# Squares in the common product tiles; 32 products left over, V1 x and V0 x of two chunk pairs together in one group

## The chip, the cores and the metric

The kernel runs on one core of a Trainium2 chip. The metric is the device time of one execution in microseconds: 444.65 us before the change (the median of three runs, 444.37, 444.65 and 445.27). Everything is float32. TensorE multiplies, VectorE (DVE), ScalarE (ACT) and GpSimd (POOL) prepare its operands and finish its results, and SyncE (SP) issues most of the DMAs.

## The reference

A compressed interaction network: three cross layers of 128 channels over F = 64 features with E = 16 numbers each, for B = 1024 examples. After the first two layers half of the channels go to the output and half go on.

```python
for i in range(n):
    z = jnp.einsum('bfe,bge->bfge', x0, h)        # x0 = x, h = x at first
    z = z.reshape(Bn, f0 * fh, e)
    y = jnp.einsum('oc,bce->boe', Ws[i], z) + bs[i][None, :, None]
    if split_half and i != n - 1:
        half = y.shape[1] // 2
        x_i, h = (y[:, :half, :], y[:, half:, :])
    else:
        x_i, h = (y, y)
    xs.append(x_i)
pooled = jnp.sum(jnp.concatenate(xs, axis=1), axis=2)
return pooled @ fc_w.T + fc_b
```

Only one number for each example comes out, so the layers collapse. The channels that go on from the first layer are h1 (64 sums of products x_f·x_g, with W0). The second and third layers together are worth, per example, the sum of h1 · (q/QS), where q are 64 sums of the same products x_f·x_g with weights M that come from V2 = fc·W2 and W1, plus a term in V1 x. The channels of the first layer that go straight to the output are x · (V0 x + cx). So a kernel needs all products x_f·x_g of a column, 64 sums of them for h1 and 64 for q, and two small 64×64 products with x itself, V1 x (it belongs to q) and V0 x.

## The kernel before, in words

**Columns and chunks.** A chunk is 32 examples × 16 numbers = 512 columns (N). There are 32 chunks; pair k is chunks 2k and 2k+1. Chunks 2, 3, 0, 1 (HEAD) start while weights are still being made, 4 and 5 are worked singly (`contract`), and the 13 pairs k = 3 to 15 follow in windows of 31 labels (SPAN) each. The q part of chunks 2 and 3 is left for the end.

**Products.** On partition p, tile t = (j, i) of a chunk holds x_f·x_g with f = (p + i) mod 64 and g = (p + 16(p//64) + 4(j+1)) mod 64, for i and j from 0 to 3. The differences g − f run over 1 to 32. So each unordered pair of two different features occurs once, those with difference 32 twice (half of their weights are set to zero), and the squares not at all. DVE makes four tiles in one instruction, `product` and `w_product` (lines L242 and L654): xa, four shifted copies of x, times xb, one shifted copy. Many xb are first copied to a PSUM bank by ACT (`second`, L568), into one of the two "y" banks.

**A pair of chunks a and b.** One 128-row tile times 64 columns of weights fills half of the array for one 512-column product; in the text a *slot* is the whole array for one such product, two matmuls side by side. For a pair the kernel does not work 4 × 16 such products, but a scheme like Strassen's and Winograd's with seven groups of eight. The operands T3, X, B21, B22 come from DVE (`make_pair`), the sums T2, T1, T4 from GpSimd (`w_mix`, L671; one of them by an accumulating DMA, L669). The groups add into banks named alpha, delta and beta (`p1_run`, `p7_run`, `w_run`, `p4_run`, `late_run`); between groups ACT copies partial sums out of a bank (`snap_p1` L682, `snap_u2` L685, `snap_p7` L688), and DVE adds them back at the end (`w_hb` L692, `w_qa` L696, `w_ha` L699), multiplies h by q (`w_uu` L702) and sums over the 16 numbers (`sums` L307).

**The extras.** What the common tiles lack is done with a tile e for each chunk, x in its lower 64 partitions (loaded a second time, `load_e`) and the squares x² in the upper ones (ACT, `square`, L178). Each chunk has
- `q_extra`: e (128 rows) times va or vb, V1 and the squares' weights for q, half a slot; scattered among the fills of a window (`first_fill`, `late_run`),
- `h_extra`: x² (64 rows) times the squares' weights for h1 (`w0ds`), 64×64, a quarter of a slot,
- `v0x`: x times v0, 64×64, a quarter of a slot; then `x_v0x` (L303) or `x_v0x_parts` (L776) on DVE.

The 64-row ones are gathered: in windows where chunk a leads (`a_leads`, every second one) `joint_squares` works the eight 64×64 products of two pairs at label 16.9 of the window, two slots with 64-row tiles. That makes six joint groups; pairs 0 and 2 have theirs in the head at label 28.1, pair 15 and chunks 2 and 3 theirs at the end (`squares`, `end_squares`).

**What sets the order.** It is written out by hand: `at(label, job)` collects jobs, and they are issued sorted by label, whatever their engine; a label is about one slot of TensorE. Each engine works its own instructions in that order and waits only for what it reads or overwrites. PSUM has eight banks in three pools: "acc" (4), "set" (2) and "y" (2). All matmuls issued through `mm` have line L540. The weights v0, va and vb are made on the chip in the head: GpSimd weighs (`weigh`, L551), DVE sums (`add_up`, L555), ACT puts the halves in place (`place`, L560).

Of the kernel before, what the change touches and what calls it, by code (L numbers as in the profile page):

```python
# [58 lines left out]
NV = 196  # L59
SQ = slice(96, 128)  # L60
# [10 lines left out]
def cin_kernel(ctx, tc, xra, xrb, wh, w0r, w1h, w2t, wx1, wx0, vec, lin, out):  # L71
# [7 lines left out]
    halves = [slice(0, F), slice(F, 128)]  # L79

# [23 lines left out]
    fcb, w0ds, fcr = vs[:, 3:4], vs[:, 4:68], vs[:, 68:196]  # L104

    misc = ps.tile([128, N], F32, tag="acc", name="misc", bufs=4)
# [22 lines left out]
    va, vb, v0 = (const_tile(n, [128, F]) for n in ("va", "vb", "v0"))  # L129
# [6 lines left out]
    xas, xbs, xxs, es = {}, {}, {}, {}  # L136
# [22 lines left out]
    def load_e(c):  # L159
        es[c] = sp.tile([128, N], F32, tag="e", name=f"e_{c}", bufs=4)  # L160
        nc.sync.dma_start(out=es[c][halves[0]], in_=xra[c, 0:F])

    def load_xx(k):
        xxs[k] = sp.tile([128, N], F32, tag="xx", name=f"xx_{k}")
        for n in range(2):
            nc.sync.dma_start(out=xxs[k][halves[n]], in_=xra[2 * k + n, 0:F])

    def copy_x(c):
        k, h, x = c // 2, halves[c % 2], xas[c][:, 0, :]
        if k not in xxs:  # L170
            xxs[k] = sp.tile([128, N], F32, tag="xx", name=f"xx_{k}")
        es[c] = sp.tile([128, N], F32, tag="e", name=f"e_{c}", bufs=4)
        nc.scalar.activation(es[c][halves[1]], x[halves[1]], AF.Square)
        nc.scalar.copy(es[c][halves[0]], x[halves[0]])
        nc.scalar.copy(xxs[k][h], x[h])

    def square(c):
        nc.scalar.activation(es[c][halves[1]], es[c][halves[0]], AF.Square)  # L178
# [32 lines left out]
    def shifted(c, j, tag):  # L211
        xbs.setdefault(c, {})[j] = ps.tile(
            [128, N], F32, tag=tag, name=f"xp_{c}_{j}", bufs=4 if tag == "acc" else 2
        )
# [10 lines left out]
    w0p = ps.tile([128, 2, NJ, F], F32, tag="set", name="w0p")  # L225
# [9 lines left out]
    def new_acc(c, n=N, tag="acc"):  # L235
        accs[c] = ps.tile([128, n], F32, tag=tag, name=f"acc_{c}", bufs=4 if tag == "acc" else 2)
# [127 lines left out]
    for n in range(2):  # L364
        pv = ps.tile([128, 512], F32, tag=("set", "y")[n], name=f"pv2_{n}")
# [13 lines left out]
    for h in range(2):  # L379
# [10 lines left out]
        ps.tile([128, N], F32, tag=tag, name=f"pm_{m}", bufs=4 if tag == "acc" else 2)  # L390
# [12 lines left out]
    pcx = ps.tile([128, 1], F32, tag="acc", name="pcx", bufs=4)  # L403
# [33 lines left out]
    xb2 = ps.tile([128, N], F32, tag="set", name=f"xp_{c2}_{NJ - 1}")  # L437
    nc.scalar.copy(xb2, xbs[c2][NJ - 1])
    xbs[c2][NJ - 1] = xb2
    for j in (0, 1):  # L440
        xb3 = ps.tile([128, N], F32, tag="y", name=f"xp_{c3}_{j}")
        nc.scalar.copy(xb3, xbs[c3][j])
        xbs[c3][j] = xb3
# [17 lines left out]
    ms = flat(msb).rearrange("p (v t g) -> p v t g", v=2, g=F)  # L461

# [8 lines left out]
    def read_columns(j, queue, half):  # L471
        queue.dma_start(
            out=ms[halves[half], 1, j * NI : (j + 1) * NI],
            in_=skewed(0, 16 * half + 4 * (j + 1), [[row, NI], [1, F]]),
        )

    def read_rows(js, queue, half):
        queue.dma_start(
            out=ms[halves[half], 0].rearrange("p (j i) g -> p j (i g)", i=NI)[:, js],
            in_=skewed(  # L480
                16 * half + 4 * (js.start + 1), 0, [[4 * row, js.stop - js.start], [1, NI * F]]
            ),
        )
# [17 lines left out]
    nc.sync.dma_start(out=va[halves[1]], in_=m_ap(0, 0, [[row + F, F], [1, F]]))  # L501
# [56 lines left out]
    def place(v, out, scale):  # L558
        for m in range(2):
            nc.scalar.activation(  # L560
                out[halves[0], 32 * m : 32 * m + 32],
                shift[halves[m], 32 * v : 32 * v + 32], AF.Identity, scale=scale,
            )


    def second(c, j):
        bank = ps.tile([128, N], F32, tag="y", name=f"xp_{c}_{j}")
        nc.scalar.copy(bank, xbs[c][j])  # L568
        xbs[c][j] = bank
# [5 lines left out]
    def q_extra(c, w, out=None):  # L575
        out = accs[c][halves[1 - c % 2]] if out is None else out[halves[c % 2]]
        mm(out, w, es[c])

    def h_extra(c, out=None, start=False):
        out = accs[c] if out is None else out  # L580
        mm(out[halves[c % 2]], w0ds[halves[1]], es[c][halves[1]], start=start)

    def new_y(k, tag):
        ys[k] = ps.tile([128, N], F32, tag=tag, name=f"y_{k}", bufs=4 if tag == "acc" else 2)

    def v0x(c, tag):
        if c // 2 not in ys:
            new_y(c // 2, tag)
        mm(ys[c // 2][halves[c % 2]], v0[halves[0]], es[c][halves[0]], start=True, stop=True)
# [22 lines left out]
    def w_bank(p, name, tag, bufs):  # L612
        if name not in p:
            p[name] = ps.tile([128, N], F32, tag=tag, name=f"{name}_{p['k']}", bufs=bufs)
        return p[name]

    def alpha(p):
        return w_bank(p, "alpha", "acc", 4)[p["A"]]

    def delta(p):  # L620
        return w_bank(p, "delta", "acc", 4)[p["O"]]

    def gamma(p):
        return w_bank(p, "alpha", "acc", 4)[p["O"]]

    def beta(p):
        return w_bank(p, "beta", "set", 2)[p["O"]]
# [53 lines left out]
    def snap_p1(p):  # L681
        nc.scalar.copy(snaps[0][p["O"]], alpha(p))  # L682

    def snap_u2(p):
        nc.scalar.activation(snaps[1][p["O"]], alpha(p), AF.Identity, bias=bh1[p["A"]])  # L685

    def snap_p7(p):
        nc.scalar.copy(snaps[2][p["A"]], delta(p))  # L688

    def w_hb(p):  # L690
        hb_ = snaps[2][p["A"]]
        nc.vector.scalar_tensor_tensor(hb_, alpha(p), bh1[p["A"]], hb_, ALU.add, ALU.add)  # L692

    def w_qa(p):
        q = snaps[0][p["O"]]
        nc.vector.tensor_tensor(q, beta(p), q, ALU.add)  # L696

    def w_ha(p):
        nc.vector.tensor_tensor(delta(p), delta(p), snaps[1][p["O"]], ALU.add)  # L699

    def w_uu(p, x, out, factor):
        nc.vector.scalar_tensor_tensor(  # L702
            uu[p[out], 0], x(p), 1.0 / QS, factor[p[out]], ALU.mult, ALU.mult
# [36 lines left out]
    def first_fill(p):  # L740
        return [(lambda: q_extra(p["a"], va, p["beta"]),)] + p4_run(p)[-LATE : -LATE // 2]
# [4 lines left out]
    def late_run(p, out=alpha, first=0, last=2 * NI):  # L746
        jobs = w_run(p, out, s4, "B22", out is gamma)[first:last]
        w = va if p["joint"] == 0 else vb
        return jobs if last < 2 * NI else jobs + [(lambda: q_extra(p["b"], w, p["alpha"]),)]

    def squares(p):
        a, b = p["a"], p["b"]
        h_extra(b, p["alpha"])
        h_extra(a, p["delta"])
        v0x(b, "set")
        v0x(a, "set")

    def joint_squares(q, p):
        a, b = q["a"], q["b"]
        h_extra(b, q["delta"], True)  # L760
        h_extra(a, q["delta"])
        v0x(b, "set")
        v0x(a, "set")
        a, b = p["a"], p["b"]
        h_extra(b, p["alpha"])
        h_extra(a, p["delta"])
        mm(p["delta"][p["A"]], v0[halves[0]], es[b][halves[0]], start=True)
        mm(p["alpha"][p["O"]], v0[halves[0]], es[a][halves[0]], start=True)

    def w_hb_squares(p):  # L770
        hb_ = snaps[2][p["A"]]
        nc.vector.tensor_tensor(hb_, p["delta"][p["A"]], hb_, ALU.add)

    def x_v0x_parts(p):
        for name, h in (("alpha", p["O"]), ("delta", p["A"])):
            nc.vector.scalar_tensor_tensor(  # L776
                uu[h, 1, :], p[name][h], cx[h], xxs[p["k"]][h], ALU.add, ALU.mult
            )
# [7 lines left out]
    def first_window(t, p, after, left):  # L786
        window(
            t, p,
            p1_run(p, GROUPS) + left[1][:1] + [(q_extra, 4, va)] + w_run(p, alpha, s2, "T2")
            + left[1][1:] + w_run(p, alpha, s1, "T3"),  # L790
            p7_run(p, GROUPS) + left[0][:1] + [(q_extra, 5, va)]
            + w_run(p, beta, wq_all, "B21", True, 2 * NI) + left[0][1:]
# [4 lines left out]
    def a_leads(t, p, before, after):  # L797
        fill = first_fill(before)
        window(
            t, p,  # L800
            p1_run(p, SECOND_ROW, False) + fill[:2] + w_run(p, alpha, s2, "T2", order=FIRST_ROW)
            + fill[2:] + w_run(p, alpha, s2, "T2", order=SECOND_ROW) + second_fill(before)
            + w_run(p, alpha, s1, "T3") + p7_run(after, FIRST_ROW),
            p7_run(p, GROUPS) + late_run(before) + w_run(p, beta, wq_all, "B21", True, 2 * NI)
            + p4_run(p)[:-LATE],
            4, 8, 15,
        )
        at(t + 16.9, joint_squares, before, p)

    def o_leads(t, p, before, after):  # L810
        last = after is None
# [5 lines left out]
            + w_run(p, beta, wq_all, "B21", True, 2 * NI)  # L817
            + (late_run(p, gamma, 0, NI) if last else p1_run(after, FIRST_ROW))
            + p4_run(p)[:-LATE],
            8, 4, 19,  # L820
        )
        if last:
            at(t + 30.2, squares, p)
# [347 lines left out]
```

## Time and profile before

| | us |
|---|---|
| runs | 444.37, 444.65, 445.27 |
| span of the profiled execution | 443.4 |
| PE busy | 439.8 (99%) |
| DVE busy | 401.4 (91%) |
| POOL busy | 371.9 (84%) |
| ACT busy | 117.7 (27%) |

The profile is of one execution. Its span goes from the first to the last instruction of the core; the time of a run has a little more around it. A line of a group names the line of the kernel, the engine, the operation and what it writes and reads by the program's tile names; "128*64 128x512" on a matmul is weights of 128 rows by 64 columns and a moving operand of 128 partitions by 512 columns. A float32 matmul leaves two records. PE is TensorE's matmul, PEld its weight load, which runs beside it.

### The profile page before, as it was taken

What the parts mean: (1) busy time and instruction counts of PE and PEld (TensorE: products, weight loads), DVE (VectorE), ACT (ScalarE), POOL (GpSimd) and SP (SyncE); (2) the same over time, 40 slices, a digit from 0 to 9 for tenths busy, and PEclk for the clock granted to TensorE, in tenths of its full rate; (3) what the DMA queues carried; (4) which work ended last, traced back from release to release, by engine and by line L of the source; (5) the groups of instructions that cost most, each with busy time, mean ns of one, the idle gap of its engine ahead of it and who ended that gap; (6) DMA issues with size and microseconds to landing.
All of it is one profiled execution on the core that took longest, in us unless ns stands there. A gap on an engine that the chain in (4) does not pass through costs nothing.

```text
span 443.4 us, 5939 instructions
## 1 busy us (share of the span) xinstructions
PE 439.8 (99%) x2228; PEld 159.0 (36%) x2228; DVE 401.4 (91%) x305; ACT 117.7 (27%) x216; POOL 371.9 (84%) x136
## 2 busy tenths in 40 slices
PE   9999999999999999999999999999999999999997
PEld 6333333336633333333333333333333333333345
DVE  4896799998998999999999999999999999999744
ACT  3155341232412123131312214131231313123211
POOL 5823898999998979899798979989798997989900
PEclk9999999999999999999999999999999999999999
DMA  8997997399769756895849868598567958592400
GB/s 283 404 373 193 359 409 290 125 324 232 269 130 342 170 189 232 179 347 119 288 145 260 268 153 307 121 313 210 182 234 186 346 119 282 189 265 71 95 1 0
DMA packets 35220, 99.86 MB, mean 225 GB/s; under 512 B 6420, under 2 KB 7220, under 8 KB 28728
## 3 DMA queue, kind: packets, MB, share of 16 engines
q1 hardware_dynamic: 31784, 84.67, 53.5%
q0 software_dynamic: 1872, 13.63, 16.8%
q10 hardware_dynamic: 1536, 1.18, 1.0%
q8 instruction: 17, 0.28, 0.3%
q14 instruction: 11, 0.09, 0.1%
HBM read 84.20 MB, written 1.64 MB: 194 GB/s over the span
## 4 chain that ended last, share of the span: by engine, by line
PE 94%; DMA 4%; SPq 1%; issue 0%; DVE 0%
PE alpha L540 43%; PE delta L540 23%; PE beta L540 11%; PE acc L540 7%; PE acc L250 4%; PE q L540 3%; DMA z<-in_w1h 3%; PE acc L283 3%; DMA z<-in_w0r 1%; SPq L143 1%; PE y L540 0%; SPq L193 0%; PE pm L396 0%; PE hx L540 0%; PE po L958 0%
## 5 line engine op out<-in xcount | busy, mean ns | idle before, releaser
L671 POOL TENSOR_TENSOR z<-z,z 128x2048 f32<-128x2048 f32 (+1 forms) x85 | 300.1, 3574 | 24.9 <-PE alpha L540 14.3
L654 DVE TENSOR_TENSOR z<-xa,xp 128x2048 f32<-128x2048 f32 x103 | 231.3, 2280 | 3.4 <-ACT xp L568 1.9
L540 PE MATMUL alpha<-z,ws 128*64 128x512 f32 x624 | 233.3, 593 | 0.0
L540 PEld LDWEIGHTS alpha<-z,ws 128*64 128x64 f32 x624 | 74.5, 137 | 89.4 <-issue 82.7
L540 PE MATMUL delta<-z,w_all 128*64 128x512 f32 x208 | 96.4, 592 | 0.0
L540 PE MATMUL alpha<-z,w_all 128*64 128x512 f32 x208 | 92.4, 592 | 0.0
L540 PE MATMUL beta<-z,w_all 128*64 128x512 f32 x208 | 91.7, 593 | 0.0
L540 PE MATMUL delta<-z,ws 128*64 128x512 f32 x208 | 91.4, 592 | 0.0
L568 ACT COPY xp<-xb 128x512 f32<-128x512 f32 x88 | 51.3, 585 | 128.5 <-DVE z L654 111.9
L242 DVE TENSOR_TENSOR z<-xa,xp 128x2048 f32<-128x2048 f32 (+2 forms) x29 | 43.3, 1546 | 2.6 <-ACT xp L568 1.7
L540 PEld LDWEIGHTS alpha<-z,w_all 128*64 128x64 f32 x208 | 28.5, 137 | 29.1 <-issue 27.7
L540 PEld LDWEIGHTS delta<-z,w_all 128*64 128x64 f32 x208 | 28.5, 137 | 28.7 <-issue 27.4
L540 PEld LDWEIGHTS delta<-z,ws 128*64 128x64 f32 x208 | 28.5, 137 | 28.6 <-issue 27.4
L540 PEld LDWEIGHTS beta<-z,w_all 128*64 128x64 f32 x208 | 28.0, 137 | 27.4 <-issue 25.7
L242 POOL TENSOR_TENSOR z<-xa,xb 128x2048 f32<-128x2048 f32 x6 | 27.3, 4569 | 11.1 <-DMA xb<-in_xrb 11.0
L540 PE MATMUL acc<-z,w_all 128*64 128x512 f32 x128 | 28.1, 592 | 0.0
L685 ACT ACTIVATE snap<-alpha,vs 64x512 f32<-64x512 f32 x13 | 8.9, 684 | 52.8 <-PE alpha L540 52.8
L250 PE MATMUL acc<-z,w_all 128*64 128x512 f32 x96 | 21.4, 596 | 0.0
L307 DVE TENSOR_REDUCE acc<-uu 128x64 f32<-128x1024 f32 (+2 forms) x19 | 19.6, 1036 | 0.2
L688 ACT COPY snap<-delta 64x512 f32<-64x512 f32 x13 | 7.5, 580 | 42.2 <-PE alpha L540 27.7
L660 DVE TENSOR_TENSOR xp<-xp,xb 128x512 f32<-128x512 f32 x26 | 18.1, 697 | 0.6
L242 POOL TENSOR_TENSOR z<-xa,xb_gps 128x512 f32<-128x512 f32 (+1 forms) x6 | 14.1, 2369 | 5.3 <-ACT xb_gps L321 4.4
(129 smaller groups left out, 368.4 us busy)
## 6 DMA issues: line engine op xcount, KB each, us to landing
xa<-in_xra SPq DMA_DIRECT2D x32, 1024.0 KB, 5.8
xb<-in_xrb SPq DMA_DIRECT2D x128, 256.0 KB, 7.6
z<-z POOLq DMA_DIRECT2D x13, 1024.0 KB, 8.1
e<-in_xra SPq DMA_DIRECT2D x28, 128.0 KB, 7.2
xx<-in_xra SPq DMA_DIRECT2D x28, 128.0 KB, 2.5
z<-in_w2t SPq DMA_DIRECT2D x2, 1024.0 KB, 11.9
z<-in_wx SPq DMA_DIRECT2D x2, 1024.0 KB, 9.9
xa<-in_xra SPq DMA_DIRECT2D x4, 256.0 KB
```

The lines of the kernel that those rows point to most:

```text
L143: queue.dma_start(out=xas[c][rows * n : rows * (n + 1), at, :], in_=bass.AP(tensor=xra.tensor, offset=c * XR * N + (at.start + rows * n) * ...
L242: engine.tensor_tensor(blocks[zs[c, j]][:, at, :], xas[c][:, at, :], xbs[c][j].unsqueeze(1).to_broadcast([128, last - first, N]), ALU.mult,)
L250: nc.tensor.matmul(accs[c][halves[i % 2]], w_all[:, j * NI + i, 0:64], blocks[zs[c, j]][:, i, :], start=(j == 0 and i < 2), stop=(j == las ...
L283: nc.tensor.matmul(accs[c][halves[1 - c % 2]], w_all[:, t, 64:128], blocks[zs[c, j]][:, i, :], start=(t == 0), stop=False, skip_group_chec ...
L307: nc.vector.tensor_reduce(acc[rows, of, k, half], uu[rows, of if at is None else at, E * half.start : E * half.stop].rearrange("p k (b e) ...
L540: nc.tensor.matmul(out, w, rhs, start=start, stop=stop, skip_group_check=True)
L568: nc.scalar.copy(bank, xbs[c][j])
L654: engine.tensor_tensor(blocks[b], xas[c], xbs[c][j].unsqueeze(1).to_broadcast([128, NI, N]), ALU.mult)
L660: nc.vector.tensor_tensor(bank, bank, xbs[p["b"]][j], ALU.add)
L671: nc.gpsimd.tensor_tensor(*(blocks[b][:, first:last] for b in (o, x, y)), ALU.subtract if in1 == "T3" else ALU.add,)
L685: nc.scalar.activation(snaps[1][p["O"]], alpha(p), AF.Identity, bias=bh1[p["A"]])
L688: nc.scalar.copy(snaps[2][p["A"]], delta(p))
```

## The change

- **Tiles.** The common tiles take g = (p + 16(p//64) + 4j + 3) mod 64. The differences now run over 0 to 31, with the squares among them (half of the weights of difference 0 are set to zero where they would count twice). What is left over is difference 32: 32 products x_d·x_{d+32}.
- **The far products.** For each pair one tile d holds, in quarters of 32 partitions, x shifted by 32 (`load_d`, `copy_d`); ACT copies it to a y bank (`far_bank`) and DVE multiplies it with xx, or with a copy xs whose halves are exchanged (`load_turned`), into d (`far_product`). Pairs with even k use xs and are called turned.
- **The extras of a pair** are V1 x twice (`along_x`, 64×64 on xx or xs), V0 x twice (64×64) and four products with d (`far`, 32×64: weights dh for h1 and dq or dqh for q). `joint_extras` does those of two pairs at label 15.9 of every second window: first the eight 64×64 ones in two slots, then the eight 32×64 ones in one. `plain_extras` does the V1 x and far ones of chunks 0, 1, 4, 5 at label 29.1, and their V0 x now stands alone at 24.1. `end_extras` does pair 15 and chunks 2 and 3 at label 6.9 of the end.
- **What goes:** the tiles e, their loads and squares, va, vb, `q_extra`, `h_extra`, `joint_squares`, `w_hb_squares`, `x_v0x_parts`, the memset of weights on DVE.
- **Banks.** PSUM banks are assigned by hand (`bank`, `pair_bank`). beta is now the other half of alpha's bank: `snap_p1` copies alpha there, and the B21 products add onto it, so there is no `w_qa`. h·q of a pair is one instruction over 128 rows (`w_uu`) where there were two over 64. Late (even) pairs collect the extras for q apart (`spare`, copied by ACT, `snap_spare`, and added by DVE, `w_qb`).
- **The head.** GpSimd fills a part of the weight tile with zeros and makes four 32×512 copies for pair 0's d before it waits for the q weights, and adds dq, dh and dqh later; v0 and v1 are placed by four ACT copies each (before, two for each of v0, va and vb); `add_up` of v0 stands 0.4 labels sooner, the product X of chunk 6 with j = 1 stands 0.8 later.

```diff
     def shift_pair(c, js):
-                at = 4 * (j + 1) + 16 * h
+                at = 4 * j + 3 + 16 * h
...
-    def load_e(c):
-        es[c] = sp.tile([128, N], F32, tag="e", name=f"e_{c}", bufs=4)
-        nc.sync.dma_start(out=es[c][halves[0]], in_=xra[c, 0:F])
+    def load_d(k):
+        if is_turned(k):
+            load_turned(k)
+        for n in range(2):
+            nc.sync.dma_start(
+                out=pair_tile(ds, "d", k)[halves[n ^ is_turned(k)]],
+                in_=xra[2 * k + n, 32 : 32 + F],
+            )
...
+    def far_bank(k):
+        xbs["d", k] = bank(f"d_{k}", "y")
+        nc.scalar.copy(xbs["d", k], ds[k])
+
+    def far_product(k):
+        x = (xds if k == 1 else xss if is_turned(k) else xxs)[k]
+        nc.vector.tensor_tensor(ds[k], xbs["d", k], x, ALU.mult)
...
     def snap_p1(p):
-        nc.scalar.copy(snaps[0][p["O"]], alpha(p))
+        nc.scalar.copy(beta(p), alpha(p))
...
-    def joint_squares(q, p):
-        a, b = q["a"], q["b"]
-        h_extra(b, q["delta"], True)
-        h_extra(a, q["delta"])
-        v0x(b, "set")
-        v0x(a, "set")
...
+    def joint_extras(q, p):
+        for r in (q, p):
+            along_x(r["b"], spare(r) if r["late"] else alpha(r), start=r["late"])
+            along_x(r["a"], beta(r))
+        for r in (q, p):
+            ys[r["k"]] = pair_bank(r, "y")
+            v0x(r["k"])
+        for r in (q, p):
+            far(r["b"], dh, 0, alpha(r) if r["late"] else spare(r), start=not r["late"])
+            far(r["a"], dh, 0, delta(r))
+        for r in (q, p):
+            far(r["b"], dqh if r["late"] else dq, 1, spare(r) if r["late"] else alpha(r))
+            far(r["a"], dq, 1, beta(r))
...
-        at(t + 16.9, joint_squares, before, p)
+        at(t + 15.9, joint_extras, before, p)
+        at(t + 24, snap_spare, p)
...
-            at(t + 1, load_e, c)
-            at(t + (10 if p["joint"] == 1 else 14), square, c)
+        early = p["k"] > 3
+        at(t - 8 if early else t + 1, load_d, p["k"])
+        far_pair(t + (6.9 if p["late"] else 17.5), p["k"])
...
-    for c in (0, 1, 4, 5):
-        at(28.1, v0x, c, "acc")
-        at(28.1, h_extra, c, None, c < 2)
-    zipped(30, [(q_extra, 0, va)], [(q_extra, 1, va)])
+    at(24.1, v0x, 0)
+    at(24.1, v0x, 2)
+    at(29.1, plain_extras)
...
-    g = (p % F + 16 * (p // F) + 4 * (t // NI + 1)) % F
+    g = (p % F + 16 * (p // F) + 4 * (t // NI) + 3) % F
```

More of the change, by code (lines that the diff above doesn't have):

```diff
@@ L168, in copy_x @@
-    def copy_x(c):
[L169 to L178, printed above, removed]
+            nc.sync.dma_start(out=pair_tile(xxs, "xx", k)[halves[n]], in_=xra[2 * k + n, 0:F])
@@ L746, in late_run @@
     def late_run(p, out=alpha, first=0, last=2 * NI):
[L747 to L754, printed above, removed]
-        v0x(b, "set")
-        v0x(a, "set")
-    def joint_squares(q, p):
-        a, b = q["a"], q["b"]
-        h_extra(b, q["delta"], True)
-        h_extra(a, q["delta"])
[L762 to L778, printed above, removed]
+        return w_run(p, out, s4, "B22", out is gamma)[first:last]
+    def joint_extras(q, p):
[11 more added lines that the diff above has]
+            far(r["a"], dq, 1, beta(r))
     def window(t, p, a_column, o_column, p1, p7, u2):
@@ L857, in last_q_weights @@
         used(msb)
-        nc.vector.memset(w_all[SQ, NT - NI, 64:128], 0.0)
     def w_sums(m):
@@ L999, in end_q, with end_extras @@
             ends[n][halves[1 - c % 2]], w_all[:, t, 64:128], blocks[z][:, t % NI, cuts[n]],
[L1000 removed]
+            start=(t == 0 and n == 0),
         )
         used(z, 0.5)
[L1004 to L1008 removed]
+    def end_extras():
+        hx = bank("hx", "y")
         hxs.append(hx)
[L1010 to L1012 removed]
+        along_x(q["b"], alpha(q))
+        along_x(q["a"], beta(q))
+        for n in range(2):
+            for c in (2, 3):
+                along_x(c, ends[n][halves[1 - c % 2]], cuts[n], start=n == 1)
+        for k, where in ((q["k"], ROLES["three"][0]), (1, "y")):
+            new_y(k, where)
+            v0x(k)
+        far(q["b"], dh, 0, spare(q), start=True)
+        far(q["a"], dh, 0, delta(q))
+        for c in (2, 3):
+            far(c, dh, 1 - c % 2, hx[halves[c % 2]], start=True)
+        far(q["b"], dq, 1, alpha(q))
+        far(q["a"], dq, 1, beta(q))
+        for n in range(2):
+            for c in (2, 3):
+                far(c, dq, c % 2, ends[n][halves[1 - c % 2]], cuts[n])
     def end_h():
```

311 lines of the change are left out of this document (187 added, 124 removed).

## The prediction

> **What bounds the kernel now.** I read the page first: shares of the engines, the granted clock, the chain that ended last.
>
> ```profile
> span 443.4 us, 5939 instructions
> ...
> PE 439.8 (99%) x2228; PEld 159.0 (36%) x2228; DVE 401.4 (91%) x305; ACT 117.7 (27%) x216; POOL 371.9 (84%) x136
> ...
> PEclk9999999999999999999999999999999999999999
> ...
> PE 94%; DMA 4%; SPq 1%; issue 0%; DVE 0%
> ```
>
> TensorE works 99% of the span at full clock, and the chain runs through it for 94%. Whether that holds at every place is told by the windows; here two neighbouring pair windows:
>
> ```profile
> 139.50:166.00 26.50, 26.50 (x126) 8.89 (x124) 25.14 (x19) 6.33 (x11) 23.79 (x10) 1.00 0.71 217
> 166.00:192.50 26.50, 26.50 (x132) 8.61 (x130) 26.24 (x19) 6.21 (x11) 24.84 (x7) 1.00 0.76 231
> ```
>
> Columns: stretch, length, busy PE, PEld, DVE, ACT, POOL, clock, DMA share, GB/s. TensorE is full in both; DVE has 53.00 − (25.14 + 26.24) = 1.62 us free in the two, POOL 53.00 − 48.63 = 4.37, ACT over 40, and the DMA engines a quarter. So TensorE's slots are the currency: a slot saved is time saved, until a helper falls behind. Then the timeline of TensorE around one joint group of extras gives the price of a slot:
>
> ```profile
> 121.58 0.59 PE L540 MATMUL alpha<-e,va 128*64 128x512 f32 x1
> ...
> 122.10 0.65 PE L540 MATMUL delta<-e,vs 64*64 64x512 f32 x2
> ...
> 122.58 0.59 PE L540 MATMUL delta<-e,vs 64*64 64x512 f32 x2
> ...
> 123.01 0.59 PE L540 MATMUL delta<-e,vs 64*64 64x512 f32 x1
> ...
> 123.03 0.59 PE L540 MATMUL delta<-e,v 64*64 64x512 f32 x1
> 123.44 0.59 PE L540 MATMUL delta<-e,vs 64*64 64x512 f32 x1
> ...
> 123.98 0.64 PE L540 MATMUL alpha<-z,ws 128*64 128x512 f32 x1
> ...
> 124.46 0.59 PE L540 MATMUL alpha<-z,ws 128*64 128x512 f32 x1
> ...
> 137.33 0.59 PE L540 MATMUL delta<-z,ws 128*64 128x512 f32 x1
> ```
>
> From 124.46 to 137.33 lie 30 steps of two records side by side: 12.87/30 = 0.429 us a step. Each matmul leaves two records, so a slot, in which the whole array works for one 512-column product, is 2 × 0.429 = 0.858 us. Four 64×64 tiles start within 0.02 us (123.01 to 123.03) and the next four follow after 0.43: they too fill one slot. Going from 128-row to 64-row matmuls costs (122.10 − 121.58) + (122.58 − 122.10) − 2 × 0.429 = 0.14, and back (123.98 − 123.44) + (124.46 − 123.98) − 0.858 = 0.16: 0.15 a switch.
>
> **The change part by part.** *The slots.* The windows of the whole span with only one tile's instructions count the extras; e, then va, then vb:
>
> ```profile
> 0.00:443.40 443.40, 45.16 (x196) 12.47 (x196) 21.06 (x36) 1.00 0.72 225
> ...
> 0.00:443.40 443.40, 22.92 (x54) 1.00 0.72 225
> ...
> 0.00:443.40 443.40, 7.15 (x14) 1.00 0.72 225
> ```
>
> The first bracket is TensorE's. Of the 196 records on e, 54 + 14 are 128-row products with va or vb (two records each; the last two chunks are cut in 384 and 128 columns, so 68 records are 32 whole products): 32 half slots, 16 slots. The other 128 records are 64 matmuls of 64×64, four to a slot: 16 slots. Together 32, two for each of 16 chunk pairs. After the change a pair has two V1 x and two v0 x (64×64: one slot) and four 32-row products (32×64, eight to a slot: half a slot): 24 slots. The tiles of z keep their number. 32 − 24 = 8 slots go, one in each of six joint groups, one in the head (pairs 0 and 2), one in the tail (pairs 15 and 1): 8 × 0.858 = 6.86 us.
>
> *The switches.* A joint group before goes 128 → 64 → 128, after 128 → 64 → 32 → 128. Six joints and the tail have one switch more each, and the head, whose v0 x now runs alone at label 24.1 and the rest at 29.1, has 5 in place of 2: ten more. The step from 64 to 32 rows is nowhere in this trace. Bounds: nothing, if only the first change drains, or one lost step of 0.43; I take the 0.15 of the rows above, since it is the same act. −6.86 + 10 × 0.15 = −5.36; by the bounds −6.86 to −2.6.
>
> *The 32-row slot.* No 32-row product stands in the steady part. Bounds a step: 0.429, if all eight tiles run together as the four 64×64 do, or 0.858, if only four do. I take 0.429, because the row nearest to it (123.01 to 123.44) shows the array packed in both directions at no loss. The upper end is a rival below.
>
> *The helpers.* Groups of lines, one operation each (behind the first bar: us in total, mean ns of one):
>
> ```profile
> L568 ACT COPY xp<-xb 128x512 f32<-128x512 f32 x88 | 51.3, 585 | 128.5 <-DVE z L654 111.9 <-DMA xb<-in_xrb 12.1 <-DVE z L242 4.3
> ...
> L660 DVE TENSOR_TENSOR xp<-xp,xb 128x512 f32<-128x512 f32 x26 | 18.1, 697 | 0.6
> ...
> L699 DVE TENSOR_TENSOR delta<-delta,snap 64x512 f32<-64x512 f32 x13 | 9.0, 695 | 0.9 <-PE delta L540 0.8
> ...
> L702 DVE SCALAR_TENSOR_TENSOR uu<-delta,snap 64x512 f32<-64x512 f32 x13 | 8.9, 688 | 0.4
> ...
> L303 DVE SCALAR_TENSOR_TENSOR uu<-y,cx,xx 128x512 f32<-128x512 f32 x10 | 7.4, 748 | 0.2
> ```
>
> Height costs DVE nothing (697 for 128 rows, 695 for 64), so merging halves pays. Per two windows DVE loses two q sums and one h sum (3 × 0.69), four half products uu against two whole (4 × 0.688 − 2 × 0.748), and one of three x·v0x (0.75): 4.1 us. It gains two far products (2 × 0.697) and one q sum for the late pair (0.695): 2.1. Net −2.0, in windows that shrink by 0.7: DVE gets freer, not tighter. ACT loses four squares and gains three copies of 0.585; it has 40 us free. DMA: turned and far tiles for the squares' tiles, 28 loads more or less at a share of 0.71; the far loads are issued nine labels sooner on SP, behind a buffer that the previous joint has freed, and are read 8 us or more after. These cost nothing as long as DVE keeps its 1.6 us of spare; if the far products alone stood uncovered, 1.4 us a double window, 8 in all.
>
> GpSimd, from the waits (total us, times, longest):
>
> ```profile
> POOL z L671 <- PE alpha L540: 14.3, 6, 2.7
> ...
> POOL z L671 <- PE delta L540: 10.1, 6, 1.9
> ...
> POOL ws L867 <- DVE w_all L505: 6.8, 1, 6.8
> ...
> PEld alpha L540 <- POOL z L671: 3.2, 4, 0.8
> ```
>
> It waits for TensorE 14.3 + 10.1 = 24.4 us, 4 in each of six double windows, because TensorE frees its blocks late; a double window shorter by 0.7 leaves 3.3 of them. Its new work in the head (a small memset, four 32-row copies, each bounded above by its 128x512 multiply below) fits in the 6.8 us in which it waits for DVE.
>
> ```profile
> L242 POOL TENSOR_TENSOR z<-xa,xb_gps 128x512 f32<-128x512 f32 x4 | 5.0, 1274 | 4.4 <-ACT xb_gps L321 4.4
> ```
>
> 4 × 1.27 = 5.1 us. Without that cover its mixes, and TensorE behind them, would be late by as much.
>
> *The new wait.* The beta products now add onto a bank half that ACT's copy (snap_p1) has to fill first; queued behind that wait on TensorE is everything. A window with two slots between the last alpha product and its reuse shows the margin:
>
> ```profile
> 214.66 0.58 ACT L682 COPY snap<-alpha 64x512 f32<-64x512 f32 x1 [2.95 <-PE delta L540]
> ...
> 216.18 0.59 PE L540 MATMUL alpha<-z,ws 128*64 128x512 f32 x1
> ```
>
> 216.18 − 215.24 = 0.94 us. The other kind of window drops from three slots of cover to two, so to about the same. One bank copy in front (0.585) still fits: nothing.
>
> *The head.* v0 x stands three slots sooner, and needs v0 sooner.
>
> ```profile
> 74.36 4.47 DVE L555 TENSOR_REDUCE shift<-z 128x32 f32<-128x2048 f32 x2
> ...
> 76.67 0.47 ACT L560 ACTIVATE v<-shift 64x32 f32<-64x32 f32 x2 [3.81 <-DVE shift L555]
> ...
> 78.75 2.28 DVE L654 TENSOR_TENSOR z<-xa,xp 128x2048 f32<-128x2048 f32 x1
> ...
> 79.52 0.64 PE L540 MATMUL y<-e,v 64*64 64x512 f32 x1
> ...
> 84.31 13.73 POOL L671 TENSOR_TENSOR z<-z,z 128x1024 f32<-128x1024 f32 x4
> ...
> 98.72 9.35 POOL L671 TENSOR_TENSOR z<-z,z 128x1024 f32<-128x1024 f32 x3
> ...
> 105.49 0.59 PE L540 MATMUL delta<-z,w_all 128*64 128x512 f32 x1
> ```
>
> TensorE gets there at 79.52 − 3 × 0.858 = 76.95. The first reduction ends at 74.36 + 2.24 = 76.6; ahead of it come two far products (+1.4) and perhaps one wait for a bank (+0.6), and a 2.28 product leaves: 76.35. Then four copies of 0.47/2, where two stood: 77.3, TensorE 0.3 late. Bounds: 0, and 2.3 if the product doesn't leave. Next, the product that ended at 78.75 + 2.28 = 81.03 moves behind the x·v0x of pairs 0 and 2 and their sums (2.7) and the far products (1.4): 85.1, and GpSimd, which took it at 84.31, starts 0.8 to 1.2 late. Of the three mixes at 98.72 two are halves, so a half takes 9.35/4 = 2.34, and the second ends about 103.4 for a TensorE read at 105.49: 2.1 in hand, 0.9 left. Nothing, barely. Head in all: −0.858 + 3 × 0.15 + 0.3 = −0.1. Tail: −0.858 + 0.15 = −0.7; its waits have over 1 us.
>
> *The sum.* Six joints × (0.858 − 0.15) = 4.25, tail 0.71, head 0.1: −5.06. The span goes from 443.4 to 438.3. The runs shown are 444.37, 444.65, 445.27, so 1.0 to 1.9 (median 1.25) lie around it: 439.6 us.
>
> **The rivals.**
>
> *A, the other side: the eight 32×64 tiles run in two rounds of four.* Place: the last slot of all eight groups (six joints, head, tail). Price: 0.858 more each, 6.9: 439.6 + 6.9 = 446.5, slower than before. It decides from 5.06/8 = 0.63 us a group. For it: no 32-row row exists here, and with 32 rows four row strips must be fed at once where two are fed now. Against: two row strips and two column halves together keep the 0.43 pace.
>
> *B, they overlap in part.* Halfway between the bounds, 0.43 more a group: 3.4, 443.0; still faster. The Trainium skill, page "TensorE: Matmul & The Clock Gate", section "Measured speedup vs the span model", speaks against the change: it gives 3.07× for four row tiles of K=32 and N=512; by it a slot would be 4/3.07 = 1.30 times as long, an estimate of 8 × 0.26 = 2.1 us and 441.7. No run here shows it; the 64-row rows show no such loss.
>
> *C, the beta wait.* If ACT is two bank copies behind, 2 × 0.585 − 0.94 = 0.23 is lost at each of 13 pairs: 3.0, 442.6. For: the copy is now on TensorE's path. Against: ACT is busy 6.3 of 26.5.
>
> *D, GpSimd becomes the bound* and the change doesn't do what it says: the slots go, the time comes back as waits for z. It has 4.0 us of waits per two windows and would have to lose all of it; only head and tail gain, 444.65 − 0.8 = 443.9, no change. For: TensorE waits for z already, 3.2 us in four places.
>
> **How the numbers follow.** Forecast 0.66, A 0.09, B 0.09, C 0.10, D 0.06. What a measurement of this kernel tells from no change is about 0.2%, 0.9 us: faster is below 443.75, slower above 445.55. Faster: 0.66, C's 0.10 and most of B: 0.83. Slower: A and a little of the worst bounds together, 0.10. Same: 0.07. The forecast's own range goes from 438.6 (switches at half price, no head wait) to 441 (switches at 0.25 each, head wait 0.7). The 80% range takes in B and C: 438.5 to 443.2.
>
> **What would show it.** Right: two windows last 0.7 us less; a joint group shows eight 32-row tiles starting within 0.05 us, the next step 0.43 later; three gaps of about 0.1 around it; TensorE still 99%. Wrong: the two steps of a 32-row group 0.6 or more apart (A, B), new waits of alpha for ACT's bank copy (C) or for z of POOL (D), a gap at v0 x near 77 of over 1 us.

## The result, and the profile after

The changed kernel takes 442.19 us (median of 5 runs, 442.02 to 443.55) against 444.70 of the kernel before (5 runs, 444.37 to 445.27): a ratio of 0.9952, interval 0.9939 to 0.9965. It is faster, by 2.5 us where 5.06 were forecast. From the page of the changed kernel, the span, the engines and the chain that ended last:

```profile
span 440.9 us, 6152 instructions
...
PE 435.3 (99%) x2296; PEld 154.9 (35%) x2296; DVE 389.2 (88%) x288; ACT 114.1 (26%) x210; POOL 378.0 (86%) x143
...
PE 71%; DMA 18%; DVE 6%; issue 3%; SPq 2%; ACT 1%; ACTq 0%; DVEq 0%
```

TensorE is still at 99%, but the chain no longer runs through it alone: DMA has 18% where it had 4%. A share of 99% cannot show a stall of two microseconds in 440; the chain can. Look first at what was forecast to pay, the joint groups. The timeline of TensorE at the first row of the first group and around the second one:

```profile
121.72 0.65 PE L598 MATMUL alpha<-xx,v 64*64 64x512 f32 x2
...
172.33 0.59 PE L598 MATMUL alpha<-z,ws 128*64 128x512 f32 x1
172.86 0.65 PE L598 MATMUL alpha<-xx,v 64*64 64x512 f32 x2
...
173.34 0.60 PE L598 MATMUL alpha<-xx,v 64*64 64x512 f32 x2
...
174.19 0.60 PE L598 MATMUL y<-xx,v 64*64 64x512 f32 x2
...
174.73 0.65 PE L598 MATMUL delta<-d,dh 32*64 32x512 f32 x2
...
174.78 0.64 PE L598 MATMUL alpha<-d,dq 32*64 32x512 f32 x1
175.21 0.59 PE L598 MATMUL delta<-d,dh 32*64 32x512 f32 x2
...
175.78 0.64 PE L598 MATMUL alpha<-z,ws 128*64 128x512 f32 x1
...
176.26 0.59 PE L598 MATMUL alpha<-z,ws 128*64 128x512 f32 x1
```

Eight 32-row tiles start between 174.73 and 174.78, the next eight 0.48 later, which is also what the 64-row tiles need behind their change of height (172.86 to 173.34) and the 128-row ones behind theirs (175.78 to 176.26). So the array takes all eight at once, and rivals A and B fall. A change costs what the step into the new height and the step behind it take beyond two plain steps of 0.429: 0.15 us from 128 to 64 rows, 0.16 from 64 to 32 (174.19 to 175.21), 0.19 from 32 to 128 (175.21 to 176.26). Two windows last 172.86 − 121.72 = 51.14 us. Before, the same distance was 173.91 − 122.10 = 51.81:

```profile
173.91 0.65 PE L540 MATMUL delta<-e,vs 64*64 64x512 f32 x2
```

That is −0.67 for a forecast of −0.71. What is missing lies ahead of the first group and behind the last. At the end the timeline of TensorE, then that of VectorE, shows a stall:

```profile
416.65 2.75 PE L598 MATMUL q<-z,w_all 128*64 128x384 f32 x16
421.12 0.65 PE L598 MATMUL alpha<-xx,v 64*64 64x512 f32 x2 [1.72 <-DVE snap L778]
```

```profile
411.28 4.48 DVE L293 TENSOR_TENSOR z<-xa,xp 128x2048 f32<-128x2048 f32 x2
419.59 0.69 DVE L227 TENSOR_TENSOR d<-d,xs 128x512 f32<-128x512 f32 x1 [3.84 <-DMA xs<-in_xra]
420.31 0.76 DVE L778 SCALAR_TENSOR_TENSOR snap<-alpha,vs,snap 64x512 f32<-64x512 f32 x1
```

In brackets stands the idle time before an instruction and what ended it. TensorE waits for `w_hb` (L778). That sum itself lacks nothing, but on VectorE it stands behind the last far product, and this one waits for its operand xs from a DMA. Three windows of the same stretch (last columns: DMA share and GB/s):

```profile
414.00:416.00 2.00, 2.00 (x14) 0.72 (x11) 1.75 (x1) 0.18 (x1) 2.00 (x2) 1.00 0.11 33
416.00:418.00 2.00, 2.00 (x16) 0.92 (x14) 0.00 (x0) 0.00 (x0) 2.00 (x1) 1.00 0.13 51
418.00:419.00 1.00, 1.00 (x10) 0.38 (x6) 0.00 (x0) 0.00 (x0) 1.00 (x1) 1.00 0.13 51
```

With everything else landed, 0.13 of sixteen DMA engines move data: two. The four loads of `load_last_d` are written with an outer dimension of two chunks. The Trainium skill, page "DMA: Bandwidth & Descriptors", section "Rules for kernel authors", says that an outermost dimension smaller than 16 confines a DMA to at most that many engines; the 0.13 agrees. But why do they run so late? SyncE's queue, its largest wait and its timeline:

```profile
SPq L194 <- PE alpha L598: 79.6, 6, 13.8
```

```profile
365.70 1.82 SPq L175 DMA_DIRECT2D xb<-in_xrb  x4
380.52 1.11 SPq L194 DMA_DIRECT2D d<-in_xra  x2
381.73 0.54 SPq L161 DMA_DIRECT2D xa<-in_xra  x1
...
395.45 2.67 SPq L202 DMA_DIRECT2D d<-in_xra  x2
398.17 3.19 SPq L202 DMA_DIRECT2D xs<-in_xra  x2
```

From 367.5 to 380.5 SyncE stands in front of the load of the last pair's d (L194), until the joint group at 377 has read the buffer, and the load of chunk 2 (381.73) stands behind it. Before, that load went out ten microseconds sooner:

```profile
371.99 0.33 SPq L143 DMA_DIRECT2D xa<-in_xra  x1
```

### The profile page after: what moved, and what is told of

It reads as the page before. It is cut to its first block, busy times and chain, and to the rows that moved or that the text cites. A ratio compares the mean times of both kernels' runs of the same rounds, so it can differ in the third digit from the quotient of the medians.

```text
span 440.9 us, 6152 instructions
## 1 busy us (share of the span) xinstructions
PE 435.3 (99%) x2296; PEld 154.9 (35%) x2296; DVE 389.2 (88%) x288; ACT 114.1 (26%) x210; POOL 378.0 (86%) x143
## 4 chain that ended last, share of the span: by engine, by line
PE 71%; DMA 18%; DVE 6%; issue 3%; SPq 2%; ACT 1%; ACTq 0%; DVEq 0%
PE alpha L598 45%; PE delta L598 20%; DMA xa<-in_xra 6%; DMA xs<-in_xra 4%; DMA z<-in_w2t 3%; PE q L598 2%; DVE z L740 2%; PE acc L598 2%; DVE z L293 2%; DMA xb<-in_xrb 2%; PE y L598 1%; DMA md<-z 1%; DMA z<-md 1%; DMA z<-in_w0r 1%; DVE shift L613 1%
## 5 line engine op out<-in xcount | busy, mean ns | idle before, releaser
L598 PE MATMUL alpha<-z,ws 128*64 128x512 f32 x616 | 228.5, 593 | 0.0
L598 PE MATMUL alpha<-z,w_all 128*64 128x512 f32 x416 | 183.5, 593 | 0.0
L598 PEld LDWEIGHTS alpha<-z,ws 128*64 128x64 f32 x616 | 71.7, 137 | 83.1 <-issue 82.7
L598 PEld LDWEIGHTS alpha<-z,w_all 128*64 128x64 f32 x416 | 56.4, 137 | 58.7 <-issue 58.1
L771 ACT ACTIVATE snap<-alpha,vs 64x512 f32<-64x512 f32 x13 | 8.9, 684 | 35.4 <-PE alpha L598 35.3
L598 PEld LDWEIGHTS acc<-z,w_all 128*64 128x64 f32 x128 | 10.6, 137 | 17.1 <-issue 16.5
L768 ACT COPY alpha<-alpha 64x512 f32<-64x512 f32 x13 | 7.3, 558 | 34.1 <-PE alpha L598 21.0
```

The source lines that it names most:

```text
L598: nc.tensor.matmul(out, w, rhs, start=start, stop=stop, skip_group_check=True)
L768: nc.scalar.copy(beta(p), alpha(p))
L771: nc.scalar.activation(p["t"][p["O"]], alpha(p), AF.Identity, bias=bh1[p["A"]])
```

## The experiments

Every kernel is the changed one with one or a few edits. The table has the median, the ratio to the kernel before in the same job, and two numbers of the profiled execution: the start of the first joint group (the head), and the time from there to the last reduction on VectorE (joint groups and end).

| kernel | us | ratio, interval | first group | to the end |
|---|---|---|---|---|
| before | 444.70 | | 122.10 | 318.88 |
| changed | 442.19 | 0.9952 (0.9939 to 0.9965) | 121.72 | 316.82 |
| tail_rows | 441.11 | 0.9917 (0.9904 to 0.9930) | 121.15 | 315.04 |
| tail_early | 441.80 | 0.9926 (0.9914 to 0.9938) | 120.70 | 316.61 |
| tail_order | 441.88 | 0.9923 (0.9911 to 0.9936) | 121.23 | 316.40 |
| head_late | 442.42 | 0.9944 (0.9928 to 0.9960) | 121.86 | 317.69 |
| d_back | 440.40 | 0.9900 (0.9885 to 0.9914) | 121.80 | 315.03 |
| v_early | 441.65 | 0.9939 (0.9926 to 0.9952) | 122.43 | 316.35 |
| all_three | 440.80 | 0.9914 (0.9902 to 0.9927) | 121.03 | 315.03 |
| switches | 441.94 | 0.9942 (0.9930 to 0.9954) | 121.94 | 316.36 |
| d_last | 440.44 | 0.9913 (0.9899 to 0.9927) | 121.17 | 315.03 |
| back_v | 440.55 | 0.9913 (0.9899 to 0.9927) | 121.56 | 315.04 |
| head_dve | 439.79 | 0.9899 (0.9883 to 0.9915) | 120.48 | 315.03 |
| back_far | 439.99 | 0.9892 (0.9875 to 0.9909) | 120.27 | 315.03 |

The last two columns come from two rows each, as here for d_last and then the changed kernel:

```profile
121.17 0.65 PE L598 MATMUL alpha<-xx,v 64*64 64x512 f32 x2
...
436.20 0.28 DVE L1176 TENSOR_REDUCE hb<-pl 2x8 f32<-2x128 f32 x1 [0.51 <-PE pl L1172]
```

```profile
438.54 0.28 DVE L1176 TENSOR_REDUCE hb<-pl 2x8 f32<-2x128 f32 x1 [0.52 <-PE pl L1172]
```

They are worth having apart: seven executions with the same head put the first group anywhere from 120.70 to 121.94 (mean 121.39), while the second column is 315.03 or 315.04 in all seven kernels whose end has no stall. The noise sits in the head, and ahead of one instruction of it, a product of VectorE at 69.08 in the changed kernel:

```profile
69.08 2.29 DVE L740 TENSOR_TENSOR z<-xa,xp 128x2048 f32<-128x2048 f32 x1 [0.66 <-ACT xp L627]
```

In the seven executions this product starts anywhere from 67.90 to 69.31, and from there to the first group it is 52.63 or 52.64 us in six of them (52.80 in tail_early, where the product came first). So the first group follows VectorE.

**tail_rows: the last d by plain rows.**

```diff
-            for h in halves:
-                nc.sync.dma_start(out=pair_tile(kept, name, 1)[h],
-                    in_=bass.AP(..., ap=[[XR * N, 2], [N, 32], [1, N]]))
+            for r in range(4):
+                nc.sync.dma_start(out=pair_tile(kept, name, 1)[32 * r : 32 * r + 32],
+                    in_=xra[2 + r % 2, first : first + 32])
```

> Theory T: the missing 1.8 us is one stall of TensorE at the end (418.91 to 421.12 in the changed kernel), because the four loads of the last d and its turned copy, each written with an outer dimension of 2, keep only two DMA engines busy and land at 419.4. Here the same rows come as eight loads of 32 plain rows. T expects them to land before 410, the stall gone, and 442.2 - 1.8 = 440.4 us. Rival I: they are late because they are issued late (395.5) behind other traffic; the shape is without effect, the stall stays, 442.2. Rival O: TensorE waits at the end for something else than these loads; landing sooner, the stall stays, 442.2.

441.11 us, and the second column falls by 1.78, to 315.04. The same windows and VectorE's far product in this kernel:

```profile
414.00:416.00 2.00, 2.00 (x14) 0.86 (x12) 1.97 (x3) 0.00 (x0) 2.00 (x2) 1.00 0.00 0
416.00:418.00 2.00, 2.00 (x14) 0.86 (x12) 1.81 (x2) 0.00 (x0) 2.00 (x1) 1.00 0.00 0
```

```profile
415.12 0.68 DVE L224 TENSOR_TENSOR d<-d,xs 128x512 f32<-128x512 f32 x1
```

Nothing is left in flight, and the product waits for nothing. O falls; I, that the shape is without effect, falls too. The median gained 1.1, by the ratios 1.6, not 1.8; the intervals do not touch.

**tail_early: the same loads at label −21 in place of −12.**

> The four loads of the last d keep their shape, but stand 9 labels sooner on SyncE's queue. T: they take as long as before but start some 8 us sooner at best, so the stall goes too, 440.4; if the queue itself holds them back until about 395 they gain little and the stall stays in part. I: 440.4 as well. O: 442.2. So with the run before it this tells shape from time of issue.

441.80: nearly nothing. SyncE issues them no sooner:

```profile
395.89 1.77 SPq L202 DMA_DIRECT2D d<-in_xra  x2
```

A label on SyncE is only a place in a queue, and ahead of that place the queue itself is late. The second column has the stall still (316.61).

**tail_order: `w_hb` ahead of the last far product on VectorE.**

```diff
-    far_pair(t - 3, 1)
+    at(t - 5.6, far_bank, 1)
+    at(t + 0.8, far_product, 1)
```

> The loads are left as they are; only VectorE's order changes: the last far product stands behind the last pair's h sum (w_hb) instead of ahead of it. T: the loads still land at 419.4, but what TensorE waits for is w_hb, which was only queued behind the product; V1 x and V0 x then cover 1.9 us and the product is there in time: stall gone or under 0.3, 440.4 to 440.7. If the far products themselves are what TensorE lacks, the stall only moves some instructions later and 442 stays.

441.88; the second column falls by 0.42 only. TensorE no longer waits for `w_hb`, but the stall has successors: a bank copy of ACT (`snap_u2`) late behind late products, and then the next load in the queue, xx of pair 1 (first row: timeline of TensorE; second: its waits near the end, in total, times, longest).

```profile
407.77 0.64 PE L598 MATMUL alpha<-z,w_all 128*64 128x512 f32 x1 [0.24 <-ACT snap L771]
```

```profile
PEld q L598 <- DMA xx<-in_xra: 0.5, 1, 0.5
```

So what was late was a whole queue of loads, not one product.

**d_back: the d loads of the odd pairs back at label 1.**

```diff
-        early = p["k"] > 3
+        early = p["late"]
```

> From the changed kernel, the d loads of the odd pairs go from label -8 back to label 1 of their window, where the loads of e stood; nothing else. In the changed kernel SyncE stands 13 us in front of each of them until the previous joint group has read the buffer, and the loads of the next chunks stand behind it. Theory Q: only at the end are those loads short of margin; there the loads of chunks 2 and 3 (xa, xb) start 9 us later than in the kernel before and fall together with the four loads of the last d. Expected: SyncE's waits for alpha at that line from 80 us to under 10, the 3.4 us in which VectorE stands still near 398 under 1.5, and the stall at the end shorter by 0.5 to 1, 441.4 us. Rival: SyncE's waits are all covered and only the two-engine loads matter: 442.2.

440.40, and an interval clear of the changed kernel's: more than theory Q expected (441.4). The stall is gone with the two-engine loads still in place, and VectorE's 3.35 us near 398 are 0.53. (Of the loads of chunks 2 and 3 only chunk 2's had been late; chunk 3's went out at 385.80 in the changed kernel, 389.70 in the kernel before.) SyncE's waits fell only from 80 to 55 us, not under 10 as expected: it now waits at the same line with the next loads already out.

**d_last: the same for the last pair alone** (`early = 3 < p["k"] < NPAIR + 2`).

> From the changed kernel, only the last pair's d (k = 15) is loaded at label 1 of its window; the other odd pairs keep label -8. Theory Q: SyncE's other waits of 13 us are covered, and the whole gain of moving all of them (442.2 to 440.4) comes from this one, since behind it stand the loads of chunks 2 and 3 and of the last d: 440.4 to 440.7 us, SyncE's waits for alpha at that line still some 70 us, no stall near 419. Rival: the waits cost a little in every pair of windows; then a sixth of the gain comes, 441.9.

440.44 and 315.03, the whole of d_back's gain; the rival's 441.9 falls. SyncE still waits 73.5 us, but the load of chunk 2 is out before:

```profile
SPq L194 <- PE alpha L598: 73.5, 6, 13.7
```

```profile
368.55 0.33 SPq L161 DMA_DIRECT2D xa<-in_xra  x1
...
379.98 1.11 SPq L194 DMA_DIRECT2D d<-in_xra  x2
```

In the steady part those waits are covered; at the end one of them costs 1.8 us. Taking away either the late start (d_last) or the narrow loads (tail_rows) removes the stall: it needed both.

**switches: V0 x behind the 32-row products, one more change of height in each joint group.**

> From the changed kernel, the joint groups in another order: V1 x, the 32-row products, then V0 x, so the height goes 128, 64, 32, 64, 128 with one change more in each of six groups. At the 0.15 us of the prediction: +0.9 us, 443.1, and the two windows 51.3 apart. If a change between 64 and 32 rows is free: 442.2. At one lost step each: +2.6, 444.8.

The time, 441.94, missed the 443.1, because in this order there is no stall at V1 x in the end: xs lands 0.24 sooner than in the changed kernel (VectorE's product starts at 419.35 instead of 419.59), and TensorE, slowed by the added changes and by a later first group, comes to V1 x 1.5 us later. The price stands in the timeline:

```profile
173.24 0.65 PE L598 MATMUL alpha<-xx,v 64*64 64x512 f32 x2
...
174.26 0.64 PE L598 MATMUL delta<-d,dh 32*64 32x512 f32 x2
...
175.31 0.65 PE L598 MATMUL y<-xx,v 64*64 64x512 f32 x2
...
176.32 0.64 PE L598 MATMUL alpha<-z,ws 128*64 128x512 f32 x1
```

The group starts 173.24 − 121.94 = 51.30 after the one before it, 0.16 more than 51.14, and so do the next two; the fourth and fifth distance are 51.48 and 51.43, which is not explained. One change more costs 0.16, with the 32-row slot left as it was. So of the 0.19 by which the third change lengthened two windows at most about 0.03 can belong to that slot itself.

**The head.** In the changed kernel VectorE sums v0 until 76.49, ACT's four copies put it in place until 77.48, and TensorE, which was due at 76.6 (nine steps of 0.429 from 72.73), starts V0 x at 77.28. GpSimd waits 1.13 us for the product X, and a weight load of TensorE then 0.25 for GpSimd:

```profile
74.21 2.28 DVE L613 TENSOR_REDUCE shift<-z 128x32 f32<-128x2048 f32 x1
```

```profile
76.52 0.96 ACT L619 ACTIVATE v<-shift 64x32 f32<-64x32 f32 x4 [6.95 <-DVE shift L613]
```

```profile
77.28 0.89 PE L598 MATMUL y<-xx,v 64*64 64x512 f32 x2 [0.49 <-ACT v L619]
```

```profile
85.72 13.75 POOL L757 TENSOR_TENSOR z<-z,z 128x1024 f32<-128x1024 f32 x4 [1.13 <-DVE z L740]
```

```profile
105.28 0.14 PEld L598 LDWEIGHTS delta<-z,w_all 128*64 128x64 f32 x1 [0.25 <-POOL z L757]
```

**head_late: V0 x of pairs 0 and 2 back at label 29, x times it at 29.9.**

> V0 x of pairs 0 and 2 goes back beside the other extras of the head (label 29 instead of 24.1), and x times it with its sums behind the product X of chunk 6. Theory H: the early place costs a wait of 0.8 us for v0 (TensorE ready at 76.6, v0's last copy ends at 77.5), two switches of 0.15, and GpSimd's 1.1 us wait for X, which comes back as 0.25 us of TensorE's waits: 1.3 us in all, 440.9 us. Rival: the wait for v0 is only passed on (the start of the kernel is what sets the head's end), no more than the switches come back, 441.9.

442.42, no gain, and 52.64 us from VectorE's product to the first group (69.22 to 121.86), as without this edit. TensorE, no longer held at V0 x, waits for v1 and then for a bank that the later x·v0x frees:

```profile
81.81 0.89 PE L598 MATMUL acc<-xx,v 64*64 64x512 f32 x2 [0.67 <-ACT v L619]
84.58 0.64 PE L598 MATMUL delta<-z,ws 128*64 128x512 f32 x1 [0.40 <-DVE uu L354]
```

**v_early: the reductions of v0 and v1 one product sooner.**

```diff
-    ... 4, 16.6, 16.7), (1, fcr[:, 64:128], 5, 20, 20.1)):
+    ... 4, 16.4, 16.45), (1, fcr[:, 64:128], 5, 16.8, 16.85)):
...
-        at(24.6, sums, k, slice(0, 128), ...
+        at(26.1, sums, k, slice(0, 128), ...
```

> From the changed kernel, the two reductions that make v0 and v1 stand one product sooner on VectorE, and the two sums of x times v0 x stand behind the product X of chunk 6. Theory H: v0 is ready at 75.3 in place of 77.5 and v1 at 79.7 in place of 81.9, so TensorE's wait of 0.8 at V0 x goes, no wait for v1 takes its place, GpSimd's wait for X (1.1) goes and with it 0.25 to 0.5 of TensorE's waits up to the first joint group: 441.2 us. Rival: the head's end is set by GpSimd's chain, and TensorE waits for its mixes what it no longer waits for v0: 442.

441.65, between the two, with the intervals of both kernels overlapping. The wait for v0 is gone, but the way from VectorE's product to the first group is 53.27 us, longer than 52.64: TensorE waits further on for VectorE and ACT:

```profile
100.34 1.04 PE L598 MATMUL alpha<-z,w_all 128*64 128x512 f32 x2 [0.32 <-DVE z L740]
101.72 0.61 PE L598 MATMUL alpha<-z,ws 128*64 128x512 f32 x1 [0.33 <-ACT snap L771]
```

**all_three: tail_rows, d_back and v_early together.**

> The three edits together: last d by plain rows, d loads of odd pairs at label 1, reductions of v0 and v1 sooner. If the three causes are apart and are all that was missing, the forecast's 439.6 us comes out, 439.3 to 440.0, with the profile's dense part of TensorE broken by nothing but changes of tile height. If a part of the missing time lies elsewhere, over 440.3.

440.80: no better than d_back alone, and over 440.3, which by what was expected means that a part of the missing time lies elsewhere.

**back_v (d_back and v_early), head_dve (the same, and pair 3's far product ten labels later), back_far (d_back and that product, without v_early).**

```diff
-        far_pair(t + (6.9 if p["late"] else 17.5), p["k"])
+        far_pair(t + (6.9 if p["late"] else 17.5 if early or p["k"] > 3 else 27), p["k"])
```

> All odd pairs' d loads at label 1, and the reductions of v0 and v1 one product sooner; the loads of the last d stay as in the changed kernel. Theory H: the head wait of 0.8 is apart from the end's and its removal shows beside it: 440.4 - 0.5 to 0.8, 439.6 to 439.9. Rival: VectorE's own chain of products sets the head's end, so TensorE only waits for a product of chunk 6 or 8 near 100 what it no longer waits for v0: 440.4.

> As back_v, and the far product of pair 3 moves from the midst of VectorE's densest stretch (near 99) ten labels later, behind that pair's last products. If VectorE's chain sets the head's end (the rival above), this takes 0.7 us out of it ahead of what TensorE waits for at 105 to 115, and with v0 on time 439.7 or less comes out, 0.5 under back_v. If GpSimd's mixes set it, no change from back_v.

> As head_dve without the sooner reductions: d loads of the odd pairs at label 1, far product of pair 3 ten labels later. If VectorE's chain alone sets the head's end, whatever v0 does, 439.8 us as in head_dve. If v0's lateness and VectorE's chain overlap, so that each hides the other and both have to go, 440.4 as in d_back and back_v, with TensorE's wait for v0 (0.3 to 0.8) still there and the stretch from V0 x to the first joint group 0.3 to 0.5 shorter than in the changed kernel at best.

440.55, 439.79 and 439.99. Twice v_early is in or out with no other difference (back_v against d_back, head_dve against back_far): +0.15 and −0.2, nothing. Twice the far product stands early or late: −0.76 and −0.41, but the intervals of the ratios overlap. The first group starts at 120.48 and 120.27, the two earliest of all, and most of that is luck: in both executions VectorE was early already at the product of 69 us, ahead of all that this edit moves, at 67.81 in head_dve and in back_far at

```profile
67.88 2.29 DVE L740 TENSOR_TENSOR z<-xa,xp 128x2048 f32<-128x2048 f32 x1 [0.66 <-ACT xp L627]
```

From there to the first group it is 52.39 us in back_far, 0.25 under 52.64, and 52.67 in head_dve, 0.11 under back_v (52.78) and 0.17 under all_three (52.84). This fits a head whose end VectorE's chain of products sets; a gain of one to a few tenths stands in these single executions, and more is not shown. TensorE's wait for v0, which back_far was expected to keep, is not there in this execution. head_dve and back_far are the fastest kernels of the study, 4.7 and 5.06 us under the kernel before in their own jobs; that 5.06 is also the forecast's sum is chance, since both hold edits that the forecast did not have.

## Why the prediction was right in direction and wrong in size

By the rows of the two profiles: the last reduction moved from 440.98 to 438.54, −2.44, where the forecast had −5.06. The joint groups and the end were to give −4.09 and the head with pair 3's own extras −0.97 (8 slots at 0.858, less switches, less the 0.3 for v0). Without a stall the groups and the end give 315.03 − 318.88 = −3.85; the stall takes 1.79 of that back; the head gave −0.38 in this execution. So 1.79 of the missing 2.62 is the stall, 0.59 the head, 0.24 the rest, for which the switches account. The 0.59 is no firm figure: by the mean of the seven executions with this head (121.39) it would be 0.26, and of the kernel before there is one execution only.

```profile
440.98 0.28 DVE L1096 TENSOR_REDUCE hb<-pl 2x8 f32<-2x128 f32 x1 [0.51 <-PE pl L1092]
```

- **The step that failed** is this one: "the far loads are issued nine labels sooner on SP, behind a buffer that the previous joint has freed, and are read 8 us or more after. These cost nothing …". By labels the joint group is done before; but SyncE, which only issues, was at that place at 367 and the group at 377. The buffer was not free, and the loads behind it were not looked at. Shown by d_back and d_last.
- **The tail**, "its waits have over 1 us", failed for the same reason and one more: the loads of the last d stand in the prediction only among "28 loads more or less"; that two engines alone would carry them was not looked at. Shown by tail_rows.
- **Slots and the 32-row slot: right.** Every joint group has three slots and the eight 32×64 tiles run together. Rivals A and B are answered by the 0.48 of 174.73 to 175.21. The Trainium skill, page "TensorE: Matmul & The Clock Gate", section "Measured speedup vs the span model", has 3.07× for four row tiles, by which the prediction estimated 0.26 us more for each 32-row slot. The trace does not agree: at most about 0.03 is left for it.
- **Luck.** The measured 442.19 lies close to the figures of C (442.6), B (443.0) and that estimate (441.7), and inside the range that was widened to take in B and C. This is chance: the time was not lost in any of these places.
- **Switches: right in kind, small in size.** 0.15 each was forecast; the third one adds 0.19 to a group (0.858 − 0.67). Seven of them outside the head, 0.04 each, make up the 0.24 and a little more (0.28).
- **VectorE: right.** Between the first and the sixth joint group its busy time fell from 50.08 to 47.89 us for two windows, 2.2, forecast 2.0 (in the whole span from 401.4 to 389.2). It was no bound in the steady part.
- **GpSimd: right.** Its waits for TensorE fell from 24.4 to 19.4 us, 3.2 in a double window where 3.3 were forecast. Rival D is out.

```profile
POOL z L757 <- PE delta L598: 11.1, 6, 2.1
...
POOL z L757 <- PE alpha L598: 8.3, 5, 1.7
```

- **The beta wait** (rival C) is not there: no wait for L768 stands among TensorE's. A neighbour of it, the copy of L771, shows up only where VectorE is late (tail_order at 407.77, v_early at 101.72).
- **The head: right mechanisms, mis-sized.** In this execution v0 came some 0.8 late, not 0.3, and GpSimd waited 1.1, where 0.8 to 1.2 was forecast. But the wait for v0 is not what the head costs. Taking it away alone gave nothing, and the first group stands 52.64 behind VectorE's product whether TensorE waits for v0 (the changed kernel) or for v1 (head_late). By these rows VectorE's chain sets the pace there, of which the prediction counted only v0 and one product. "Nothing, barely" was two small waits too generous: 0.25 each at 105.28 and 112.14.

## What to carry to other kernels

Read a moved DMA from where its queue stands in time, not from the label it is given: an issuing queue runs ahead until it meets a buffer that isn't free, and then everything behind it is late. Look for that lateness where the stream ends, because the steady part covers it. When a median moves by less than its noise, measure from a landmark behind the place where the noise arises. When an engine is 99% busy, the chain that ended last and a split of the span at a fixed landmark find a stall that no share shows.

## What the runs showed of the hardware

- Eight 32×64 tiles of float32 with 512 columns start within 0.05 us, and the next eight 0.48 later, as four 64×64 ones do behind a change of height. A change from 64 to 32 rows costs what one from 128 to 64 does, about 0.15 us; the one from 32 back to 128 cost 0.19.
- Loads whose outer dimension is two ran on two of sixteen DMA engines, at 51 GB/s for both together; the same rows in plain loads were landed by 414 where the others took until 419.
